# A tuned attention and expert block on one core: the 512 small turns of the maxima become float32r products with an identity

## The chip, the cores and the metric

The kernel runs on one core of a Trainium2 chip. A core has five engines that run side by side, each with its own queue: TensorE (matrix products; PE in the profile, with PEld for its weight loads), VectorE (DVE), ScalarE (ACT), GpSimd (POOL) and SyncE (SP, which here only issues transfers). A product takes a stationary operand, which is loaded into the array first ("LDWEIGHTS"), and a moving operand that streams through it; it writes to PSUM, a small memory of eight banks, from which ACT or DVE must take the values before the bank is free again.

The metric is the device time of one execution in microseconds. The kernel before takes 2659.15 us, the median of three runs (2658.19 to 2659.2).

## The reference

For 32 sequences of 512 tokens with 256 channels, the block computes a two-step causal attention with 16 heads of 16 channels, adds the input, normalizes, runs a gated layer of 8 experts, and normalizes again. The part that matters here:

```python
qk = x @ W_attn + b_attn
q, k = (qk[..., :C], qk[..., C:])            # and per head
y = _causal_attn(q, k, v)                    # v is x itself
e = v[:, :, 1:, :] - y[:, :, :-1, :]
k2 = x[:, :-1] @ W_k2 + b_k2                 # per head
y2 = _causal_attn(q[:, :, 1:, :], k2, e)
...
x = _layernorm(x + proj(y) + proj(y2))
x = _layernorm(x + _L0_ffn_ref(x, ...))
```

`_causal_attn` is a softmax over the keys up to the query's own place. The experts' router names tokens of the first sequence only, so only that sequence has expert work; the others pass through two normalizations.

## The kernel before

**Groups and steps.** The work is cut into groups `n` of four heads of one sequence, 4 groups a sequence and 128 in all. The loop over `step(n)` overlaps several groups: in step n the row maxima of group n, the transposed scores of groups n-1 and n-2, the weighted sums of group n-2 and the normalization of group n-3.

**Maxima and scores.** `maxima` (L267 to L323) forms the scores query by key in PSUM (`sm`, L297), masks them by products with `pick` and `hide` (L282), and DVE takes each row's largest (`top`, L321). `halve` (L325) splits `top` into a float32r part and a float32r remainder and writes both into `mx`, a tile with 128 queries on the partitions and 4 heads x 32 slots along the free dimension. `augment` (L330) turns `mx` for the four blocks of 128 queries into one PSUM bank `mt` with four transposes (L334: `mx` is the stationary operand, `ident` the moving one), and ACT copies the bank to `m` (L336). `scores` (L349) forms the scores again, key by query (`sc`, L361), with three float32r products a part: two halves of the queries, and `m` with `minus`, which subtracts the maximum. ACT takes the exponential (`pt`, L378) and POOL clears the masked corner (L382). `values` (L422) multiplies `pt` with the values (`av`, L430), ACT copies it (`avs`, L438), and `normalize` (L440) turns it with float32 transposes (`yt`, L445).

**A float32r value** is a float32 value rounded so that one pass of a product takes it; `half(ap)` only reads a tile under that type. `sm` and `sc` are products of such values, four row groups of 32 partitions at a time, one a head. The projections (`pj` L219, `po` L522), the experts (`gu` L603, `dn` L626) and `av` are full float32 products, and each has two records in the profile.

**Order.** The program puts TensorE and SyncE under a manual schedule: their queues hold what the code emits, in that order. The order on ACT, DVE and POOL is arranged by a scheduler when the program is built. A step has five slots; `slot(n, u)` interleaves the `sc` and `sm` products of two pairs of heads, first those of pair 1 and then those of pair 0, and behind each slot come the closures in `rest[u]`. `augment(n - 1)` stands behind slot 0. What follows it there is a projection for a later group (`pj`, 256 columns) or `attended` (`po`), whose result DVE adds to the residual (`h`, L525). In 8 steps the second gate product of an expert (`gu`, from `hidden(e - 1, 1, 0)`) stands ahead of it; DVE adds its bias (`hf`, L611), ACT takes a tanh (`sig`, L615) and DVE multiplies (`sig`, L616).

**PSUM.** Single banks have one tag and four buffers (`bank`), which go round in the order in which the code asks for them. Slot 0 takes four for `sc`; then `mt` takes the first of these again and `pj` or `po` the second. The `sc` tiles of slot 1 take the last two, and then those of `mt` and `pj` or `po`. A product into a bank waits until the last reader of the bank's earlier contents is done.

Of the kernel before, what the change touches and what calls it, by code (L numbers as in the profile page):

```python
# [9 lines left out]
F32 = mybir.dt.float32  # L10
# [7 lines left out]
P = 128  # L18
# [16 lines left out]
def half(ap):  # L35
    return ap.bitcast(F32R)
# [3 lines left out]
def block_kernel(  # L40
# [16 lines left out]
    nc = tc.nc  # L57
# [10 lines left out]
    const = ctx.enter_context(tc.tile_pool(name="const", bufs=1))  # L68
# [10 lines left out]
    def bank(name):  # L79
        return psum.tile([P, T], F32, tag="one", name=name, bufs=4)  # L80
# [60 lines left out]

    ident = const.tile([P, P], F32, name="ident")
    make_identity(nc, ident)
    mhalf = const.tile([P, NB], F32, name="mhalf")
    nc.gpsimd.memset(mhalf, -0.5)

# [31 lines left out]
    mx = [const.tile([P, NB, GH, HS], F32, name=f"mx{i}") for i in range(2)]  # L178
# [146 lines left out]
    def halve(n):  # L325
        t, top = mx[n % 2], groups[n]["top"]
        nc.vector.tensor_copy(half(t[:, :, :, 0:2]), top)
        nc.vector.tensor_sub(half(t[:, :, :, 2:4]), top, t[:, :, :, 0:2])

    def augment(n):  # L330
        d = groups[n]
        ps = bank(f"mt{n}")
        for i in range(NB):
            nc.tensor.transpose(ps[:, i * P : (i + 1) * P], mx[n % 2][:, i].rearrange("p h s -> p (h s)"), ident)  # L334
        d["m"] = grp.tile([P, T], F32, tag="m", name=f"m{n}")
        nc.scalar.copy(half(d["m"]), ps)  # L336

# [312 lines left out]
    def step(n):  # L650
# [13 lines left out]
        if ready(n - 1):  # L664
            rest[0].append(lambda: augment(n - 1))
# [148 lines left out]
```

## Time and profile before

| | |
|---|---|
| median of three runs | 2659.15 us |
| profiled execution | 2655.88 us, of which the span from the first to the last instruction is 2654.2 us |
| mean granted TensorE clock | 0.990 |
| the four transposes of a group (L334) | 512 loads and 512 products, one record each |
| load, product of a transpose, median | 140 ns, 273 ns |
| ACT's copy of `mt` (L336) | 128, median 617 ns |
| who held TensorE ahead of `mt` | ACT's exponential (L378), 126 times, 25.9 us in all |
| who waited for the transposes | ACT's copy L336, 10 times, 19.0 us in all |

A line of the groups view reads: line, engine, operation, output<-inputs, shape, count, then busy time in us and the mean of one in ns, then the engine's idle time ahead of these instructions and who ended it. `128*128` is rows by columns of the array, and `f32` stands there for float32 and float32r operands alike. A line of the timeline reads: start and length in us, engine, line, operation, count, and in brackets the idle time ahead. Neighbours that are alike are merged, so the length of a merged line runs from the first start to the last end. The profile's engine times are records: matmuls are pipelined and a record lasts longer than the time for which the array is held.

### The profile page before, as it was taken

Reading aid. Unit: us, or ns where it says so; the run is one execution under the profiler, and the core shown is the slowest. Engines: PE = TensorE matmul, PEld = TensorE weight load, DVE = VectorE, ACT = ScalarE, POOL = GpSimd, SP = SyncE. Lnnn points to the kernel's source line nnn. Section 1 sums busy time; section 2 is a strip of 40 time slices with the busy share of each in tenths; the row PEclk is TensorE's granted clock in tenths of the full one; section 3 lists DMA queues with packets and bytes.
Section 4 is the critical chain, followed back from the end, with each engine's and each line's share of the span. In section 5 each row is a group of like instructions: output and inputs, shape, how many; then the busy total and the mean of one; then the engine's idle time right before and its main releaser. Section 6 shows DMA issues by size and latency. Waiting matters only on the chain.

```text
span 2654.2 us, 98011 instructions
## 1 busy us (share of the span) xinstructions
PE 2593.7 (98%) x41488; PEld 1800.0 (68%) x41488; DVE 1936.3 (73%) x3225; ACT 1757.9 (66%) x3416; POOL 1730.8 (65%) x3303
## 2 busy tenths in 40 slices
PE   7999999999999999999999999999999999999997
PEld 4666666667676666666677667666776767677765
DVE  6767777677777777777777777777777777777773
ACT  3766544467667766766776677676777667677774
POOL 4555555466666667666666666666766666676664
PEclk8999999999999999999999999999999999999998
DMA  5323233233333333333333333342333334333320
GB/s 142 88 75 85 73 89 95 70 85 102 81 92 87 93 94 82 102 84 83 96 86 101 82 97 89 75 105 82 99 88 93 93 75 104 82 90 96 88 67 25
DMA packets 167461, 233.26 MB, mean 88 GB/s; under 512 B 21528, under 2 KB 91152, under 8 KB 167024
## 3 DMA queue, kind: packets, MB, share of 16 engines
q1 hardware_dynamic: 164592, 226.54, 32.9%
q8 instruction: 329, 5.39, 0.9%
q14 instruction: 108, 0.88, 0.1%
q10 hardware_dynamic: 2368, 0.42, 0.1%
q0 software_dynamic: 64, 0.02, 0.0%
HBM read 75.41 MB, written 16.78 MB: 35 GB/s over the span
## 4 chain that ended last, share of the span: by engine, by line
PE 90%; ACT 5%; issue 2%; DVE 2%; POOL 1%; DMA 0%; ACTq 0%; POOLq 0%; SPq 0%; DVEq 0%
PE av L430 22%; PE sc L361 20%; PE pj L219 13%; PE sm L297 10%; PE sm L282 7%; PE yt L445 6%; ACT pt L378 5%; PE po L522 4%; PE mt L334 3%; PE gu L603 2%; PE ys L511 1%; PE dn L626 1%; DVE top L321 1%; POOL xr L503 0%; POOL h L544 0%
## 5 line engine op out<-in xcount | busy, mean ns | idle before, releaser
L321 DVE TENSOR_REDUCE top<-sm 128x2 f32<-128x768 f32 (+3 forms) x1800 | 1536.4, 907 | 611.2 <-PE sm L297 610.6
L378 ACT ACTIVATE pt<-sc 128x512 f32<-128x512 f32 (+1 forms) x2564 | 1323.8, 601 | 333.8 <-PE sc L361 198.0
L382 POOL TENSOR_SCALAR_AFFINE_SELECT pt<-pt 128x256 f32<-128x256 f32 x2048 | 789.9, 410 | 520.2 <-ACT pt L378 519.8
L297 PE MATMUL sm<-kk_t,q_t 32*128 32x512 f32 (+2 forms) x7168 | 1100.0, 382 | 16.7 <-DVE top L321 9.3
L361 PE MATMUL sc<-q_t,kk_t 32*128 32x256 f32 (+3 forms) x8192 | 1028.2, 334 | 3.0 <-DVE h L525 1.8
L361 PEld LDWEIGHTS sc<-q_t,kk_t 32*128 32x128 f32 x8192 | 678.5, 184 | 257.5 <-issue 160.2
L361 PE MATMUL sc<-m,minus 32*128 32x256 f32 (+3 forms) x4096 | 694.6, 318 | 0.0
L297 PEld LDWEIGHTS sm<-kk_t,q_t 32*128 32x128 f32 x7168 | 567.6, 185 | 23.1 <-DVE top L321 12.2
L282 PE MATMUL sm<-hide,pick 32*128 32x64 bf16 (+5 forms) x10240 | 517.7, 217 | 0.0
L361 PEld LDWEIGHTS sc<-m,minus 32*128 32x128 f32 x4096 | 441.2, 185 | 10.0
L219 PE MATMUL pj<-xT,wq_sb 128*128 128x256 f32 (+1 forms) x1020 | 397.7, 513 | 6.3 <-DVE wq_sb L112 6.3
L438 ACT COPY avs<-av 128x512 f32<-128x512 f32 x256 | 150.4, 588 | 324.7 <-PE av L430 324.7
L430 PE MATMUL av<-pt,e_pad 128*32 128x512 f32 (+3 forms) x4096 | 304.3, 437 | 7.5 <-ACT pt L378 0.8
L430 PE MATMUL av<-pt,v_pad 128*32 128x512 f32 (+3 forms) x4096 | 302.7, 435 | 8.3 <-POOL pt L382 5.0
L231 ACT ACTIVATE pk<-pj,bp_qk 128x256 f32<-128x256 f32 (+1 forms) x255 | 151.3, 593 | 190.3 <-PE pj L219 182.7
L237 POOL TENSOR_TENSOR pk<-pk,lead 128x512 fp32r<-128x512 f32 x192 | 244.9, 1276 | 14.3 <-ACT lead L236 3.6
L430 PEld LDWEIGHTS av<-pt,v_pad 128*32 128x32 f32 x4096 | 136.3, 109 | 163.0 <-issue 126.9
L282 PEld LDWEIGHTS <-pick 32*128 32x128 bf16 x10240 | 243.7, 93 | 0.9 <-issue 0.7
L219 PEld LDWEIGHTS pj<-xT,wq_sb 128*128 128x128 f32 x1020 | 175.5, 192 | 92.1 <-issue 64.3
L430 PEld LDWEIGHTS av<-pt,e_pad 128*32 128x32 f32 x4096 | 128.9, 110 | 144.0 <-issue 135.6
L474 POOL TENSOR_TENSOR y<-y,y 128x256 f32<-128x256 f32 x128 | 96.6, 755 | 125.4 <-DVE mv L538 58.0
L445 PE MATMUL yt<-ident,avs 128*128 128x128 f32 x1024 | 168.0, 287 | 6.0 <-ACT pt L378 1.0
(90 smaller groups left out, 1955.1 us busy)
## 6 DMA issues: line engine op xcount, KB each, us to landing
q_t<-lead SPq DMA_DIRECT2D x256, 128.0 KB
q_t<-pk SPq DMA_DIRECT2D x256, 128.0 KB
kk_t<-lead SPq DMA_DIRECT2D x256, 128.0 KB
kk_t<-pk SPq DMA_DIRECT2D x256, 128.0 KB
xT<-in_xT SPq DMA_DIRECT2D x32, 512.0 KB
x<-in_x SPq DMA_DIRECT2D x32, 512.0 KB
xr<-in_x SPq DMA_DIRECT2D x32, 512.0 KB
out<-h SPq DMA_DIRECT2D x31, 512.0 KB
```

The lines of the kernel that those rows point to most:

```text
L219: nc.tensor.matmul(ps[:, 0 : hi - lo], wq_sb[:, m, c, part * P : (part + 1) * P], seqs[b]["xT"][:, c, lo:hi], start=(c == 0), stop=(c == N ...
L231: nc.scalar.activation(pk[:, lo:hi], ps[:, 0 : hi - lo], AF.Identity, bias=bp_qk[:, m, part : part + 1])
L237: nc.gpsimd.tensor_sub(half(pk), pk, lead)
L282: nc.tensor.matmul(ps[hh][:, 0 if alone else hh].rearrange("p (k c) -> p k c", c=P)[:, first::step, HS * c :], pick[rows, c], hide[rows, c ...
L297: nc.tensor.matmul(part(ps[hh], i, na, at)[:, 0 if alone else hh], half(d["q"][rows, k, i * P : (i + 1) * P]), half(d["kk"][rows, a : a + ...
L321: nc.vector.tensor_reduce(to, view, AX.X, ALU.max)
L361: nc.tensor.matmul(ps[hh][:, at * P : at * P + T - j * P], half(keys), half(queries[:, j * P :]), start=(k == 0), stop=(k == 2),)
L378: nc.scalar.activation(pt[:, hh, lo:hi], ps[hh][:, lo:hi], AF.Exp, scale=HD**-0.5)
L382: nc.gpsimd.affine_select(diag, diag, pattern=[[0, NH2], [1, P]], compare_op=ALU.is_ge, fill=0.0, base=-a, channel_multiplier=-1,)
L430: nc.tensor.matmul(ps[HS * h : HS * (h + 1), j * P :], vals[:, j, (g * GH + h) * HV : (g * GH + h) * HV + HS], d["pt", a, j, h // NH2][:, ...
L438: nc.scalar.copy(avs, ps)
L445: nc.tensor.transpose(ps[:, i * P : (i + 1) * P], d["avs", a][:, i * P : (i + 1) * P], ident)
```

## The change

`ident` is copied once to a float32r tile, and the four transposes of `augment` become ordinary products: `mx`, read as float32r, stays the stationary operand, and the float32r identity is the moving one. Since `mx` holds float32r values and the identity ones and zeros, `mt` holds the same values. Nothing else is edited.

```diff
     ident = const.tile([P, P], F32, name="ident")
     make_identity(nc, ident)
+    ident_half = const.tile([P, P], F32, name="ident_half")
+    nc.vector.tensor_copy(half(ident_half), ident)
     mhalf = const.tile([P, NB], F32, name="mhalf")
...
         for i in range(NB):
-            nc.tensor.transpose(ps[:, i * P : (i + 1) * P], mx[n % 2][:, i].rearrange("p h s -> p (h s)"), ident)
+            nc.tensor.matmul(
+                ps[:, i * P : (i + 1) * P],
+                half(mx[n % 2][:, i].rearrange("p h s -> p (h s)")),
+                half(ident_half),
+                start=True,
+                stop=True,
+            )
         d["m"] = grp.tile([P, T], F32, tag="m", name=f"m{n}")
         nc.scalar.copy(half(d["m"]), ps)
```

## The prediction

> **What bounds the kernel now.** I read the page's busy line first, then the chain of waits, then the groups by shape, and last the timeline of single stretches.
>
> ```profile
> PE 2593.7 (98%) x41488; PEld 1800.0 (68%) x41488; DVE 1936.3 (73%) x3225; ACT 1757.9 (66%) x3416; POOL 1730.8 (65%) x3303
> ...
> PE 90%; ACT 5%; issue 2%; DVE 2%; POOL 1%; DMA 0%; ACTq 0%; POOLq 0%; SPq 0%; DVEq 0%
> ```
>
> TensorE is busy 98% of the span and holds 90% of the chain; the clock row stands at 9 in all but the first and last slices, so there is no clock to win or lose. TensorE sets the end, but 98% does not mean that it streams all the time, since records overlap and their ends are modelled. What matters is the distance from one start to the next, and who releases the next weight load. So the change is priced in three places: the four instructions themselves, the load that follows them, and the order on the engines that a scheduler arranges.
>
> **The four products (L334, 128 groups of 4).** From the groups by shape, weight loads first, then matmuls (the number after the comma is the mean of one in ns):
>
> ```profile
> L361 PEld LDWEIGHTS sc<-m,minus 32*128 32x128 f32 x4096 | 441.2, 185 | 10.0
> ...
> L334 PEld LDWEIGHTS mt<-ident,mx 128*128 128x128 f32 x512 | 54.9, 142 | 29.4 <-ACT pt L378 25.5 <-issue 3.9
> ```
> ```profile
> 1004.95 0.22 PE L361 MATMUL sc<-q_t,kk_t 32*128 32x128 f32 x1
> ```
> ```profile
> 311.86 0.36 PEld L334 LDWEIGHTS mt<-ident,mx 128*128 128x128 f32 x3 [0.29 <-issue]
> ```
>
> `sc` is a float32r product with 128 stationary columns, so its load (185 ns) is what the new loads will be; the transpose's load takes 142. A lone 128-column float32r matmul is recorded at 0.22 us, the transpose's median is 0.273 us. One form is about 45 ns slower in the load, the other about 50 ns slower in the stream. Which of them sets the distance between starts is seen in two timelines. After an expert's product the last three transpose loads span 0.36 us (at 311.86), so they start (0.36-0.14)/2 = 0.11 us apart, and there the load is hidden and the stream sets it. For float32r, two loads of the same rows in a row start 0.10 to 0.11 us apart (1011.10 and 1011.20 below); there the load sets it. So transposes: load about 0.06, then four streams of 0.11, done at about 0.49 us after the first load's start. float32r: four loads of 0.11 and a last stream of 0.055, done at 0.44+0.055 = 0.49 us. The sum is zero for the group.
>
> Two rules of the Trainium skill differ from this. "TensorE: Matmul & The Clock Gate", Back-to-back issue gap, gives N/2.4+2.5 ns, 56 ns at 128 columns, for a product whose weights are there: the change would then win 512 x (109-56) ns = 27 us. The rows above say that the load, at 0.11 us, is longer than the product, so I take the rows: 0. "Perfetto Trace Analysis", Transposes, tells to use a transpose and not a standard matmul, since transposes have logic that skips the arithmetic; by that the change loses, with no figure given. The rows give the transpose the shorter load and the longer stream, and no loss.
>
> **The load behind the group.** In an ordinary step (ACT, then weight loads):
>
> ```profile
> 1008.90 2.06 ACT L378 ACTIVATE pt<-sc 128x512 f32<-128x512 f32 x4 [0.29 <-PE sm L297]
> ```
> ```profile
> 1009.55 0.42 PEld L334 LDWEIGHTS mt<-ident,mx 128*128 128x128 f32 x4 [0.20 <-ACT pt L378]
> 1010.03 0.73 PEld L522 LDWEIGHTS po<-wp_sb,ysT 128*128 128x128 f32 x4
> 1011.10 0.18 PEld L361 LDWEIGHTS sc<-q_t,kk_t 32*128 32x128 f32 x2 [0.33 <-ACT pt L378]
> ...
> 1011.20 0.19 PEld L361 LDWEIGHTS sc<-q_t,kk_t 32*128 32x128 f32 x2
> ```
>
> The four exponentials follow each other at (2.06-0.60)/3 = 0.49 us and end at 1009.50, 1009.99, 1010.47 and 1010.96. `mt` starts 0.05 us after the first of them and `po` 0.04 us after the second: both want a PSUM bank that an exponential frees. So the group begins and the next product begins when ACT says so, 0.48 us apart. The new group can let the next load go when its fourth product starts, at 0.44 us; the transposes could at 0.39. Both are before 0.48. In about 120 of the 128 groups the change is worth 0, and a faster product would be worth nothing either. In the 8 groups behind an expert's product the new spacing (110 against 109 ns) costs some 4 ns each: 0.
>
> Bounds: if loads and streams did not overlap, four products would take 4 x 0.16 = 0.64 us against 0.48, +0.16 us x 120 = +19 us. If the load with a wait could only start about 0.09 us behind the fourth product's true start (the gap with which `mt`'s first load follows the end of the row-tiled streams before it, a stream's end being its record's less the 0.16 us by which a 0.22 us record outlasts 128 columns), it would go at 0.53 instead of 0.48: +0.05 x 120 = +6.5 us. From below it is 0, since ACT holds both ends. I take 0, as the float32r rows overlap.
>
> **ident_half (one DVE copy at the start).** The nearest row is the copy of `minus`, 0.23 us. It stands in DVE's queue at about 11.6 us, ahead of a `wq_sb` copy that is first used at 26.6 us; DVE idles from 16.7 to 19.3 us waiting for POOL. 0; without that cover 0.2 us.
>
> **The order on ACT and DVE.** Order on TensorE and SP is written by hand and is the same in both built programs, but for the operand. The scheduler places the other engines' work anew, and in the 8 steps that run an expert's second gate product it moves ACT's copy of `mt` (L336) behind the expert's tanh `sig` (L615), and in four of them also DVE's `h` (L525) behind DVE's `sig` (L616). POOL's order is unchanged. This is the part with a price. One step of each kind before, first with `po`, ACT, DVE and loads, then with `pj`:
>
> ```profile
> 312.50 0.59 ACT L336 CAST m<-mt 128x512 fp32r<-128x512 f32 x1 [1.11 <-PE mt L334]
> 312.98 0.64 ACT L615 ACTIVATE sig<-hf 128x512 f32<-128x512 f32 x1
> ```
> ```profile
> 312.14 0.75 DVE L611 TENSOR_SCALAR hf<-gu,b_gu_sb 128x512 f32<-128x512 f32 x1
> 313.37 0.42 DVE L525 TENSOR_TENSOR h<-po,xr 128x256 f32<-128x256 f32 x1 [0.48 <-PE po L522]
> 313.71 0.68 DVE L616 SCALAR_TENSOR_TENSOR sig<-sig,hf 128x512 f32<-128x512 f32 x1
> ```
> ```profile
> 313.83 0.24 PEld L361 LDWEIGHTS sc<-q_t,kk_t 32*128 32x128 f32 x4
> ...
> 315.01 0.30 PEld L603 LDWEIGHTS gu<-x1T,gu 128*128 128x128 f32 x2
> ```
> ```profile
> 282.95 0.59 ACT L336 CAST m<-mt 128x512 fp32r<-128x512 f32 x1 [1.06 <-PE mt L334]
> 283.44 0.63 ACT L615 ACTIVATE sig<-hf 128x512 f32<-128x512 f32 x1
> 283.97 0.47 ACT L231 ACTIVATE pk<-pj,bp_qk 128x256 f32<-128x256 f32 x1
> ```
>
> Four banks go round. In such a step the second pair of `sc` products (pair 0) takes the banks of `mt` and of `po` or `pj`, so it waits for `m` and for `h` or `pk`. With `po`: `h` ends at 313.79, and the loads stand at 313.83. After the change ACT's `sig` starts when `hf` is done (312.89+0.05), ends at 313.58; DVE's `sig` starts some 0.05 later and ends at 314.31; `h` overlaps it by 0.08 as now, and ends at 314.65. The `sc` load moves from 313.85 to 314.70, and its product, now at 314.06 behind other streams, to 314.81: +0.75 us. TensorE takes products in order and stands still for that time. Of it some 0.05 is slack, since the next `gu` load waits for an exponential until 315.01: +0.7 us. With `pj`: `sig` 283.40 to 284.03, `m` to 284.52, `pk` from 284.41 to 284.88 instead of 284.44: +0.44 us, without slack. `m` itself is used only a slot later.
>
> Sum: 4 x 0.7 + 4 x 0.44 = 4.6 us. Behind these stretches comes some 4 us of TensorE work that waits for nothing delayed, so nothing is caught up: I take +4.5 us. Bounds: 0, if the copies slip without holding the banks' next user; 8 x 0.9 = 7 us, if every step pays the whole delay.
>
> **Sum.** The profiled execution has a span of 2654.2 us and 2655.88 us as a whole; 2655.88 + 0 + 0 + 4.5 = 2660.4. The runs' median is 2659.15, 3.3 us above the profiled one, so on that scale the forecast is 2663.6 us, +0.17%. About 0.2% (5.3 us) is what a measurement of this kernel tells from no change: the forecast is inside it, near its upper edge.
>
> **Rivals.**
> - *The group holds up the next load* (slower). The load behind the group waits for the fourth product's true start plus 0.09 us: +6.5 us, with the reordering +11: 2670. For it: such a gap of 0.09 us stands ahead of `mt`, behind row-tiled work. Against it: `po` follows the exponential by 0.04 us, which leaves no room for a gap of TensorE's own. It decides as soon as the group needs more than 0.48 us. Chance 0.25 (loads in series, +24 us or more, being 0.05 of it).
> - *The product is really shorter and TensorE's time counts* (faster). With 56 ns a product and no ACT release, -27+4.5: 2637. For it: TensorE has 90% of the chain. Against it: the releases by ACT at both ends, and the 0.11 us loads. It decides only if a 128-column float32r load takes under 0.1 us and the exponentials end early. Chance 0.06.
> - *The scheduler's order costs nothing*, the stall is caught up or lies under another wait: 2659. For it: `m` is not due for a slot. Against it: the loads that stand 0.04 us behind `h`, and `pk`. Chance 0.14.
> - *The forecast*: 0.55, with 2661 to 2667 as its own range.
>
> Range: from below 2659 (0, with the measurement's spread) to the slower rival and a little more, 2656 to 2673. Faster by over 0.2%: 0.06. Slower by over 0.2% (above 2664.5): 0.25 from the rival and 0.2 of the forecast's upper part, 0.45. Within: 0.49.
>
> **What would show it.** Right: `mt` loads at about 185 ns and matmuls near 220 to 330 ns, `po` and `pj` still 0.05 us behind the second exponential, step length equal outside the expert stretch (about 260 to 500 us), and there `sc` loads 0.4 to 0.9 us later in 8 places. Wrong: ordinary steps that are longer or shorter by 0.05 us or more, or `sc` behind `m` with no delay in the expert steps.

## The result, and the profile after

Over 12 runs each the changed kernel takes 2660.97 us (median; 2656.14 to 2663.67) and the kernel before 2656.24 us (2652.0 to 2661.17). The ratio is 1.0018, 95% interval 1.0010 to 1.0027: 4.7 us slower, where the forecast had 4.5. The interval goes from 2.7 to 7.2 us, so the runs alone bound the size only loosely. The profiled execution takes 2659.52 us.

From the page of the changed kernel, busy time by engine:

```profile
PE 2598.4 (98%) x41488; PEld 1810.4 (68%) x41488; DVE 1938.0 (73%) x3226; ACT 1757.8 (66%) x3416; POOL 1726.1 (65%) x3303
```

Shares and counts are as before, and TensorE's share of the chain of waits is 89% (90% before), so the page alone doesn't say what happened: DVE has one instruction more, and PEld is busy 10 us longer. The view of the tile `mt` shows the four products, lengths in ns as smallest, median and largest:

```profile
L337 PEld LDWEIGHTS mt<-ident_half,mx x512: 186/192/333, 38.6 to 2608.4; 128*128 128x128 f32 x171
L337 PE MATMUL mt<-ident_half,mx x512: 272/275/623, 38.6 to 2608.5; 128*128 128x128 f32 x171
```

The load went from 140 to 192 ns. The matmul's record did not become shorter (273 ns before), although a lone 128-column float32r matmul is recorded at 0.22 us. With the loads 0.11 us apart, some 0.05 us of each record would be the wait for its own load; that is inferred from the distances, not shown by itself. An ordinary step of the changed kernel, weight loads and ACT:

```profile
1016.74 0.52 PEld L337 LDWEIGHTS mt<-ident_half,mx 128*128 128x128 f32 x4 [0.20 <-ACT pt L387]
1017.22 0.73 PEld L531 LDWEIGHTS po<-wp_sb,ysT 128*128 128x128 f32 x4
```
```profile
1016.08 2.07 ACT L387 ACTIVATE pt<-sc 128x512 f32<-128x512 f32 x4 [0.29 <-PE sm L299]
```

Four loads in 0.52 us are (0.52-0.19)/3 = 0.11 us apart, and `po` starts 0.48 us behind `mt`, as before, because the second exponential ends at 1017.17. Nothing is won or lost here. Now an expert step with `po`: ACT, DVE, and the loads of the second `sc` pair and of the next `gu`:

```profile
314.81 0.63 ACT L624 ACTIVATE sig<-hf 128x512 f32<-128x512 f32 x1 [1.55 <-DVE hf L620]
315.34 0.57 ACT L345 CAST m<-mt 128x512 fp32r<-128x512 f32 x1
```
```profile
314.02 0.75 DVE L620 TENSOR_SCALAR hf<-gu,b_gu_sb 128x512 f32<-128x512 f32 x1
315.47 0.69 DVE L625 SCALAR_TENSOR_TENSOR sig<-sig,hf 128x512 f32<-128x512 f32 x1 [0.70 <-ACT sig L624]
316.08 0.42 DVE L534 TENSOR_TENSOR h<-po,xr 128x256 f32<-128x256 f32 x1
```
```profile
313.32 0.19 PEld L337 LDWEIGHTS mt<-ident_half,mx 128*128 128x128 f32 x1 [0.24 <-ACT pt L387]
...
316.55 0.18 PEld L370 LDWEIGHTS sc<-q_t,kk_t 32*128 32x128 f32 x2 [0.41 <-DVE h L534]
...
317.55 0.30 PEld L612 LDWEIGHTS gu<-x1T,gu 128*128 128x128 f32 x2
```

ACT stands idle for 1.55 us where it copied `mt` before, DVE waits 0.70 us for the tanh that `sig` needs while `h` stands behind it, and the loads wait 0.41 us for `h`. The next `gu` comes 317.55-313.32 = 4.23 us behind the first `mt` load; before it was 315.01-311.44 = 3.57 us, with this first `mt` load:

```profile
311.44 0.14 PEld L334 LDWEIGHTS mt<-ident,mx 128*128 128x128 f32 x1 [0.24 <-ACT pt L378]
```

The spans differ by 3.6 us, and both executions had a mean granted clock of 0.990. But their clocks dipped in different places. A pair of stretches from the end of each (length, busy times, then the granted TensorE clock, DMA share, GB/s), first of before, then of after:

```profile
2624.80:2635.00 10.20, 9.94 (x67) 5.60 (x62) 1.54 (x5) 4.01 (x10) 3.81 (x8) 0.50 0.00 1
```
```profile
2632.60:2642.80 10.20, 7.31 (x76) 4.68 (x73) 2.39 (x8) 5.19 (x12) 4.40 (x9) 1.00 0.01 2
```

The kernel before had 10 us at half clock there, where the changed one had the full clock. Cut into parts, the changed execution is 1.6 us longer up to the first `av` product, 4.0 us in the 8 expert steps, 1.7 us in the 8 steps behind these, and 0.6 us in the rest of the steps, and 4.2 us shorter behind the last group's first `av` product. The parts where the dips differ thus move by as much as the expert steps do, so from here on stretches without such a dip are compared.

### The profile page after: what moved, and what is told of

The parts are those of the page before. It is cut to its first block, busy times and chain, and to the rows that moved or that the text cites. A ratio compares the mean times of both kernels' runs of the same rounds, so it can differ in the third digit from the quotient of the medians.

```text
span 2657.8 us, 98012 instructions
## 1 busy us (share of the span) xinstructions
PE 2598.4 (98%) x41488; PEld 1810.4 (68%) x41488; DVE 1938.0 (73%) x3226; ACT 1757.8 (66%) x3416; POOL 1726.1 (65%) x3303
## 4 chain that ended last, share of the span: by engine, by line
PE 89%; ACT 5%; DVE 2%; issue 2%; POOL 1%; DMA 0%; ACTq 0%; SPq 0%; POOLq 0%; DVEq 0%
PE av L439 22%; PE sc L370 19%; PE pj L221 13%; PE sm L299 10%; PE sm L284 7%; PE yt L454 6%; ACT pt L387 4%; PE po L531 4%; PE mt L337 3%; PE gu L612 2%; PE ys L520 1%; PE dn L635 1%; DVE top L323 1%; DMA xr<-in_x 0%; DVE h L534 0%
```

## The experiments

Theory A, from the forecast: the four products cost nothing, and the price is the new order on ACT and DVE in 8 steps. Theory B: the float32r products cost it themselves. Two times are read from each trace: the mean of 90 ordinary steps (groups 26 to 116), and the 8 expert steps in question (groups 10 to 18), both from the start of the first `av` product of one group to that of another. For the expert steps these starts are, before and then after:

```profile
260.43 2.36 PE L430 MATMUL av<-pt,v_pad 128*32 128x512 f32 x32
498.71 2.36 PE L430 MATMUL av<-pt,v_pad 128*32 128x512 f32 x32
```
```profile
261.91 2.36 PE L439 MATMUL av<-pt,v_pad 128*32 128x512 f32 x32
504.15 2.36 PE L439 MATMUL av<-pt,v_pad 128*32 128x512 f32 x32
```

| | ratio to before (95%) | ordinary step, ns | 8 expert steps, us |
|---|---|---|---|
| before | 1 | 19429 | 238.28 |
| after, profiled with the result | 1.0018 (1.0010 to 1.0027) | 19436 | 242.24 |
| e0_after_again | 1.0017 (1.0010 to 1.0023) | 19434 | 242.22 |
| e1_product_old_order | 1.0005 (0.9997 to 1.0013) | 19435 | 238.02 |
| e11, the same again | 1.0009 (1.0001 to 1.0017) | 19430 | 238.06 |
| e2_transpose_new_order | 1.0005 (0.9997 to 1.0013) | 19434 | 242.62 |
| e12, the same again | 1.0019 (1.0011 to 1.0026) | 19429 | 242.58 |
| e3_transposes_twice | 1.0140 (1.0124 to 1.0155) | 19780 | 241.44 |
| e4_products_twice | 1.0186 (1.0169 to 1.0203) | 19850 | 241.56 |
| e5_plain_float32 | 1.0183 (1.0168 to 1.0199) | 19849 | 241.61 |
| e6_transpose_behind_po | 0.9985 (0.9975 to 0.9994) | 19394 | 239.88 |
| e8_transpose_behind_plain | 0.9970 (0.9959 to 0.9982) | 19390 | 238.22 |
| e9_all_turns_behind | 1.0053 (1.0041 to 1.0066) | 19582 | 237.96 |
| e10_products_behind_plain | 0.9981 (0.9975 to 0.9988) | 19387 | 237.98 |

### The change once more

No edit.

> The changed kernel once more, as the yardstick for its two neighbours. Both theories: 1.0018 of the kernel before, within 0.1%. Theory A (the price is the order on ACT and DVE) puts it into the expert stretch: the time from the sixth to the fourteenth group that follows an expert's product is some 4 us longer than before, and an ordinary step is equal within 10 ns. Theory B (the float32r products themselves cost it) spreads it: 37 ns in each of 128 groups.

1.0017, and 242.22 us for the expert steps, 3.9 more than before. An ordinary step is equal within 6 ns, and 6 ns is also the distance between two traces of one kernel (e1 and e11). B's 37 ns a group are not there.

### The products with the order of before

```diff
+    late = {}
+
+    def behind(later, earlier):
+        tc.add_manual_dep(
+            later.ins,
+            earlier.ins.name,
+            mybir.DependencyInfo(mybir.DependencyClass.NoSync, mybir.DependencyReason.DATA),
+        )
...
-        nc.scalar.copy(half(d["m"]), ps)
+        copied = nc.scalar.copy(half(d["m"]), ps)
+        if "sig" in late:
+            behind(late["sig"][0], copied)
...
-        nc.vector.tensor_add(s["h"][:, i], ps[:, 0:C], s["xr"][:, i])
+        added = nc.vector.tensor_add(s["h"][:, i], ps[:, 0:C], s["xr"][:, i])
+        if "sig" in late:
+            behind(late["sig"][1], added)
```

`behind` fixes only the order of issue on one engine. `late["sig"]` holds ACT's tanh and DVE's `sig` of the expert in this step, and `added` is the `h` of `attended`.

> The changed kernel, with the expert's tanh put behind the copy of mt on ACT and DVE's sig behind h, so that ACT and DVE have the order of before but for the one copy of the identity. A: 1.0000 to 1.0005 of before; the second sc pair's load in the 8 expert steps stands again at 2.40 to 2.60 us behind the first mt load, and only about 7 ns a group are left, 1 us in all. B: 1.0018 as the changed kernel.

The order on ACT and DVE is that of before, but for the copy of the identity. The 8 steps take 238.02 us, and an expert step has its old shape (DVE, with `h` first again):

```profile
317.46 0.42 DVE L545 TENSOR_TENSOR h<-po,xr 128x256 f32<-128x256 f32 x1 [0.49 <-PE po L542]
317.80 0.68 DVE L638 SCALAR_TENSOR_TENSOR sig<-sig,hf 128x512 f32<-128x512 f32 x1
```

In that step the next `gu` comes 3.58 us behind the first `mt` load, as before. So 242.22-238.02 = 4.2 us of the expert stretch go with the order and not with the product.

### The transposes with the new order

The mirror image: the kernel before with `behind(copied, late["sig"][0])` and `behind(added, late["sig"][1])`.

> The kernel before, with its transposes, with ACT's copy of mt put behind the tanh and h behind DVE's sig, as the changed kernel has them. A: 1.0015 (4 us), with the second sc pair's loads at 3.0 us (pj) and 3.2 us (po) behind the first mt load. B: 1.0000.

242.62 us, the full price without a single float32r turn. DVE and loads:

```profile
317.06 0.69 DVE L629 SCALAR_TENSOR_TENSOR sig<-sig,hf 128x512 f32<-128x512 f32 x1 [0.69 <-ACT sig L628]
317.67 0.42 DVE L536 TENSOR_TENSOR h<-po,xr 128x256 f32<-128x256 f32 x1
```
```profile
318.14 0.18 PEld L372 LDWEIGHTS sc<-q_t,kk_t 32*128 32x128 f32 x2 [0.40 <-DVE h L536]
```

The wait of 0.40 us for `h` is that of the changed kernel, and the next `gu` again comes 4.23 us behind the first `mt` load. But the ratio of the runs, 1.0005, missed the expected 1.0015 and was the same as for the products in the old order, so the runs alone told nothing apart. Both were run again:

> The float32r products with the order of before once more, since the intervals of the first pair (1.0005, 0.9997 to 1.0013, for both) do not tell A from B, while their traces put 4.3 us on the expert stretch of the transposes with the new order and none on this one. A: under 1.0005 with the runs taken together, and 238.0 us for the 8 expert steps. B: 1.0018 and no difference in that stretch.

> The transposes with the order of after once more. A: 1.0010 to 1.0018 with the runs taken together, and 242.2 to 242.6 us for the 8 expert steps. B: 1.0000 and 238.3 us.

The transposes in the new order now came to 1.0019, the products in the old order to 1.0009. The traces repeated themselves within 0.04 us (238.06 and 242.58), so what the order costs is shown in its place by four traces. Of the ratios, the mean of the two readings of each kernel is 1.0012 for the order, as expected, and 1.0007 for the product, where under 1.0005 was expected.

That remainder goes with the clock. Each run lists its own mean granted clock, and among runs of one kernel a clock lower by 0.001 goes with 1.4 us more (a straight line through 251 runs, with the mean of each set of runs taken out; 1.3 to 1.6 at 95%). The products in the old order had mean clocks 0.0013 (e1) and 0.0014 (e11) below the runs of the kernel before beside them; the transposes in the new order lay 0.0017 above (e2) and 0.0003 below (e12). With that line taken out, the mean times stand above the kernel before as follows. This is worked out from the runs, not measured at an equal clock.

| | above the kernel before, clock taken out, us (95%) |
|---|---|
| the change (e0) | 4.3 (3.5 to 5.0) |
| the order alone (e2, e12) | 3.7 (2.8 to 4.7), 4.4 (3.5 to 5.3) |
| the product alone (e1, e11) | 0.1 (-0.9 to 1.0), 0.4 (-0.5 to 1.4) |

Runs and traces then say the same: A holds, and B is left with nothing that can be told from no change.

### The turns made twice

```diff
-        for i in range(NB):
+        for i in list(range(NB)) * 2:
```

once in the kernel before and once in the changed one. Here, in the next experiment and in e10, `behind` holds ACT and DVE to the order of before, as in e1.

> The kernel before, with the four transposes of each group made twice into the same bank. Order elsewhere as before. If four take 4 x 0.109 us of TensorE and 0.09 us of that lay under the wait for the second exponential, each of some 120 groups costs 0.34 us and each of 8 costs 0.44: +44 us, 1.0166.

> The float32r products made twice, with the order of before on ACT and DVE. A (the load sets 0.11 us a product, and the load behind the group has only 0.04 us of cover left): 0.40 us a group, +50 us, 1.019, that is 7 us more than the transposes twice. The rule of 56 ns a product: 8 products are done in 0.56 us, and the step is as long as before: under +10 us, 1.003.

An ordinary step is 351 ns longer with transposes (0.34 expected) and 421 ns with products (0.40 expected). Loads of both, first transposes, then products:

```profile
1005.63 0.85 PEld L343 LDWEIGHTS mt<-ident,mx 128*128 128x128 f32 x8 [0.20 <-ACT pt L389]
1006.46 0.73 PEld L219 LDWEIGHTS pj<-xT,wq_sb 128*128 128x128 f32 x4
```
```profile
1016.31 0.97 PEld L346 LDWEIGHTS mt<-ident_half,mx 128*128 128x128 f32 x8 [0.19 <-ACT pt L398]
1017.20 0.74 PEld L221 LDWEIGHTS pj<-xT,wq_sb 128*128 128x128 f32 x4
```

The next product's first load comes 0.83 and 0.89 us behind the first `mt` load. With eight turns the exponential no longer hides the end, and the products are seen to be the slower form by 0.06 us a group. Most of it comes at the start: the second load follows the first by 0.11 us with products and by 0.06 us with transposes, and from there on both forms go about 0.11 us a load (112 and 109 ns, medians). So the change does have a cost on TensorE in this place, and in the kernel it lies under the wait. As for 56 ns a product, eight of them would have been done in 0.56 us; they took 0.89. The ratio 1.0140 of the doubled transposes (1.0124 to 1.0155) missed the expected 1.0166, although the step was as expected. Its four runs had a mean clock of 0.9925 against 0.9901 of those before; by the line above that is 3.4 us, about half of what is missing.

### An ordinary float32 product

```diff
-            nc.tensor.transpose(ps[:, i * P : (i + 1) * P], mx[n % 2][:, i].rearrange("p h s -> p (h s)"), ident)
+            nc.tensor.matmul(
+                ps[:, i * P : (i + 1) * P], mx[n % 2][:, i].rearrange("p h s -> p (h s)"), ident, start=True, stop=True
+            )
```

> The transposes replaced by ordinary float32 products with the identity, order as before. Two records a product[...]: 8 x 0.11 us and a longer last stream, 0.40 us a group beyond the wait: +45 to +55 us, 1.019. If an ordinary product is as cheap as a transpose whatever the type: 1.000.

1.0183, 420 ns a step: two records for each product, as many as the float32r products made twice, and the same price. The advice of the Trainium skill ("Perfetto Trace Analysis", Transposes) to use a transpose and not a standard matmul thus holds here for plain float32, by 0.42 us a group; for values that are float32r already, the step of this kernel is the same with either.

### The turn behind the long product

In the old place exponentials hold both ends of the group. If that is so, the group is better off behind `pj` or `po`, whose streams hide its wait and its first load.

```diff
-        if ready(n - 1):
-            rest[0].append(lambda: augment(n - 1))
...
+        if ready(n - 1):
+            rest[0].append(lambda: augment(n - 1))
         for s in range(len(units)):
             slot(n, s)
```

The new lines come after everything else that the step appends to `rest[0]`.

> The kernel before with augment behind the projection or output product of slot 0 instead of ahead of it. If ACT's exponentials release both the first and the second bank (A), the long product hides the second release and the weight load of the turns: 0.04 us less a step in about 115 steps, 0.998 of before. If TensorE's own time sets the pace, 1.0000. If the copy of mt comes too late for slot 1, slower.

0.9985, and 35 ns less in each ordinary step; but the 8 expert steps lost 1.6 us. So the move was made only where no expert runs (`n < n_all and not 0 <= n - first_expert <= E`):

> The kernel before with augment behind the long product of slot 0, but only in steps without an expert; the expert steps keep their order. If the exponentials hold both ends of the old place, each of some 110 steps is 0.035 us shorter, as in the trace of the earlier run with the move in all steps, and the 1.6 us that its expert steps lost are not lost: 0.9980 to 0.9985 of before.

0.9970 (0.9959 to 0.9982), the fastest kernel of the study, with transposes; its step is 39 ns shorter and its expert stretch as before. The 39 ns in some 110 steps are 4.3 us, 0.16%, so the 0.30% is more than the move explains, and better than the 0.9980 to 0.9985 expected. Its six runs had a mean clock of 0.9923 against 0.9902 of those before; with the clock taken out as above, they are 5.5 us faster (4.1 to 6.8), which the steps nearly cover. Its loads:

```profile
1013.08 0.73 PEld L522 LDWEIGHTS po<-wp_sb,ysT 128*128 128x128 f32 x4 [0.19 <-ACT pt L378]
1013.84 0.57 PEld L334 LDWEIGHTS mt<-ident,mx 128*128 128x128 f32 x4
1014.58 0.18 PEld L361 LDWEIGHTS sc<-q_t,kk_t 32*128 32x128 f32 x2 [0.17 <-ACT pt L378]
```

Only `po` waits for an exponential now; `mt` doesn't. The next `sc` waits 0.17 us instead of 0.33. With the float32r products in the same place, and the same order on every engine:

> The float32r products in the place of e8 and with its order on every engine. There the first load is hidden by the product ahead, and no exponential holds the end. If load and stream only change places (0.11 us a product either way), within 10 ns a step of e8, 1 us in all. The rule of 56 ns a product: 0.2 us a group less than e8, 24 us. If the next load has lost its cover: up to 0.05 us a group more, 6 us.

```profile
1012.22 0.63 PEld L346 LDWEIGHTS mt<-ident_half,mx 128*128 128x128 f32 x4
1012.92 0.19 PEld L381 LDWEIGHTS sc<-q_t,kk_t 32*128 32x128 f32 x2
```

The step is 3 ns shorter than with transposes (19387 against 19390), as the first of the three forecasts had it. The next `sc` load comes 0.70 us behind the first `mt` load, with transposes 0.74: here the products let go 0.04 us earlier. The step gains nothing by it, since the `av` loads behind slot 1 stand where they stood, within 0.01 us; what takes the 0.04 us back was not followed. Its ratio, 0.9981 (0.9975 to 0.9988), beats the kernel before too. With the clock taken out it is 5.3 us faster (4.5 to 6.2), the same as with transposes.

### All turns behind

The same for the turns of `normalize`, which went to the end of slots 2 and 3 in those steps.

> The same, and the turns of normalize (yt) behind the projection or output product of slots 2 and 3 too, in the steps without an expert. If their wait for an exponential is hidden in the same way: another 0.04 us in each of some 220 places, 0.995 of before. If y and e_pad, which DVE and POOL make behind them, come late for av, slower than the run with augment alone.

Slower, 1.0053, and 153 ns a step in the mean: every second step is 0.34 us longer than before, the others are not longer. The expected way, `av` late for `e_pad`, is not what happened. The weight loads of `av` do wait for POOL 105 times in this trace, 22.2 us in all, but TensorE loses next to nothing there: in the steps that are longer it is 11.73 us from the first `v_pad` load to the first `e_pad` load (11.72 before), and 3.38 us from the first load behind slot 0 to the next `v_pad` load, as in e8. The 0.34 us lie between the last `av` load and the first load behind slot 0 (2.60 us, 2.24 before), and there `sm` waits for DVE. From the view of waits (total us, times, longest), before and then this run:

```profile
DVE rden L459 <- PE yt L445: 17.6, 2, 12.2
PEld sm L297 <- DVE top L321: 12.2, 7, 4.2
```
```profile
DVE rden L459 <- PE yt L445: 116.8, 117, 11.1
PEld sm L297 <- DVE top L321: 25.2, 62, 4.2
```

DVE now stands 117 times for the later turns with `rden`, 116.8 us in all, and maxima come behind it. In one such step (from 1357 us) the last two `top` of a group start 1.2 us later than in e8, behind `den`, `rden` and `y`, and `sm` needs the banks that `top` reads. `m` has only ACT's copy behind it and a slot of time; the values of `yt` go through DVE, ahead of the maxima.

## Why the prediction was right

- **The four products, 0.** Shown. Ordinary steps of transposes and of products both read 19429 to 19436 ns. In the median of the 128 groups the transposes' loads start at 0, 0.06, 0.17 and 0.28 us, the products' at 0, 0.11, 0.22 and 0.33 us, and the next load at 0.48 us in both. Two terms that the prediction gives without a row hold as well: 0.06 us for a transpose's first load (58 ns), and 0.055 us for a float32r stream (the records of `sc<-m,minus` grow by 56 to 59 ns for each 128 columns: 277, 333 and 392 ns at 256, 384 and 512). The 56 ns of the Trainium skill ("TensorE: Matmul & The Clock Gate", Back-to-back issue gap) were not seen, and that section says itself that the formula leaves out the load and gives 81 ns for a stream of load and matmul pairs. Here, with a new load for each float32r product, it was 109 to 112 ns.
- **The load behind the group, 0.** Shown: 0.48 us behind `mt` in both kernels. The cover left for the products, 0.04 us by the prediction, is small, and that it sufficed was close; made twice, they lose 0.07 us a step more than transposes made twice.
- **The order, +4.5 us.** Right in mechanism, place and size. The term was 0.70 us for a step with `po` and 0.44 with `pj`; measured, step by step between the traces of before and after, 0.64 to 0.66 and 0.40 to 0.42. One `pj` step shows 0.13 instead, since in the trace of before its `hf` was late already (it starts 1.05 us behind the first `mt` load, 0.70 us in the other `pj` steps). Between the two traces with the products the eight come to 4.2 us against the 4.6 worked out.
- **ident_half, 0.** Not tried alone; the step times can't show it. In the trace the copy takes 0.22 us, and DVE's wait of 2.60 us for POOL stands behind it.
- **The clock.** "No clock to win or lose" was too simple: the row of tenths shows neither the short dips nor that the mean clock of a set of runs can move its time by as much as the change does.
- **Rivals.** The group did not hold up the next load in the kernel; made twice, it does (0.83 and 0.89 us). A product of 56 ns did not show. That the scheduler's order costs nothing is refuted by the traces of e2 and e12.
- **The median.** 4.7 us above the kernel before, where 4.5 was forecast. That the two agree so closely is partly luck, as the interval is 2.7 to 7.2 us; the traces have 4.0 us in the expert steps. In absolute time it is 2660.97 against the 2663.6 named, since the kernel before, in its 12 runs, stood 2.9 us below its first three.

## What to carry to other kernels

Before pricing a changed instruction, look at what releases it and what releases the one behind it: here both were exponentials, and neither form could win. A change of one operand's type can make a scheduler reorder engines that it doesn't touch; compare the built orders, and follow each moved instruction to the buffer that it frees. Where two waits on the same engine frame a short group, put a long one that is released by the first ahead of it, if nobody waits closely for the short one's result; look also at what else stands in the queue of the engine that reads this result. Where a change is as small as the spread of the runs, compare the clocks of the runs before their medians.

## What was not expected of the hardware

The clock of TensorE dips to half for stretches of about 3.4 us or a few of them: in the first 60 us, near 140 us, near 235 to 245 us or both, near 519 to 544 us and in the last 30 us, in two of the fourteen traces also between 260 and 271 us. Two traces of one kernel differ in it: e1 has 6.8 us at half clock near 141 us and 10.2 near 523, e11 has none near 141, 6.8 near 237 and 6.8 near 527. The mean clock of a run accounts for over half of the variance of the times within a kernel: the standard deviation falls from 2.2 to 1.5 us when the line is taken out. The clock's part in a single run is thus 1.7 us, against an effect of some 4 us.

Whether the form of the turns moves the clock stays open. Between 30 and 62 us the granted clock was 0.78 to 0.83 in five traces with transposes (before, e2, e12, e6, e8) and 0.71 to 0.75 in five with products (after, e0, e1, e11, e10), but 0.74 in e9, which has transposes too. Over whole runs, the five sets with float32r products that can be set against runs of the kernel before beside them (e0, e1, e4, e10, e11) lay below these, by 0.0001 to 0.0014; but e2 and e12, which are one kernel, lay 0.0020 apart by the same measure. No run separates the two.
